# A selective-scan kernel: the positive part of softplus from half sums held in PSUM, and two copies, the sums' chain and the background pace moved

## The chip, the cores and the metric

The kernel runs on one core of a Trainium2 chip. A core has a matrix engine (TensorE, "PE" in the profile; its weight loads are "PEld"), a vector engine (VectorE, "DVE"), a scalar engine (ScalarE, "ACT"), GpSimd ("POOL"), and SyncE ("SP"), which issues the DMAs here. Each engine runs its own queue in order; semaphores make one wait for another. Matmuls write to PSUM, eight banks of 2 KB for each of 128 partitions; GpSimd and DMAs work on SBUF alone in this kernel. The metric is the device time of one execution in microseconds (us), lower is better.

## The reference, cut to what matters

The input is 16 images of 64 x 64 pixels with 96 channels. Layer 0 normalizes, upsamples with a Fourier filter, applies a 96 to 384 to 96 network with a quadratic activation and goes back. Layer 1 is a four-directional selective scan over the pixels, and nearly all of the time is its scan:

```
xz = x @ in_proj_w.T;  xc, z = split(xz);  z = silu(z)
xc = silu(conv3x3(xc))                       # depthwise
x_dbl = einsum(xs, x_proj_weight)            # 4 directions: dts (6), Bs (16), Cs (16) a pixel
dts   = einsum(dts, dt_projs_weight)
delta = softplus(dts + dt_projs_bias)
h_t   = exp(delta_t * A) * h_(t-1) + (delta_t * u_t) * B_t      # 16 states a channel
y_t   = sum over states of h_t * C_t, plus u_t * D
out   = layernorm(y over directions) * z, projected
```

The change touches `delta`: softplus(s) = max(s, 0) + ln(1 + exp(-|s|)).

## The kernel before, in words

The whole program is one long list of instructions whose order is written out by hand. First `front(0)` (layer 0 and the convolutions of image 0) runs by itself, then `scan()` runs over all 16 images, then `finish(15)` by itself. Inside `scan()`, the `front` of the next image and the `finish` of the image before (norm, gate and projection) are dealt out in small pieces, as background.

**Units.** An image has 8 steps: 4 pieces of 1024 pixels forward (`pair` 0), then the same 4 backward (`pair` 1). A step has 6 blocks (`bi`), a block has 4 units (`j`). So there are 192 units an image and 3072 in all. A unit has two halves, `e` = 1 ("odd") and `e` = 0 ("even"), each of 128 partitions x 1024 pixels (32 channels x 4 states). For unit n the loop in `scan()` emits, in this order:

- the odd scan `recur(n, 1)` on VectorE (L836 forward, L838 backward), then for j < 3 the next odd decay, `decay(n + 1, 1)`: exp(delta x A) on ScalarE (L821) into the PSUM tile `da1`
- `slot(0)`: position 0
- for j = 3 the odd half's product with C on VectorE (L968), the copy of the last state (L844) and the odd decay; for j < 3 that product on GpSimd (L977)
- the issue of the stores of `yt`, if a block has ended
- the drive b = (delta u) B of unit n + 2 on GpSimd (L827)
- the even scan `recur(n, 0)`, in place in the PSUM tile `da0`
- `read_out(n - 1)`: the sum over states on TensorE (L861, 8 matmuls a half) into the one PSUM bank `y`; a backward block starts that bank with L853
- `slot(1)`: position 1
- the even half's product on VectorE (L988), the copy of the state on ScalarE (L844), the next even decay `decay(n + 1, 0)` on ScalarE, which reuses `da0` and so waits for L988
- when unit n - 1 ended a block: `store(n - 1)` copies `y` to `yt` on ScalarE (L872)
- `slot(2)`: position 2

So a block has 12 positions (3 slots x 4 units), numbered 0 to 11. Each slot calls one piece of `block_work` and then at most one step of the background.

**The sums.** `block_work` runs one `task` a block. It makes `delta` and `dtu` = delta x u for 512 pixels. L683 multiplies `dtw_s` with `pr`, giving s in the PSUM tile `s`. ScalarE makes e = exp(-|s|) (L686, L687), m = relu(s) (L689), w = 1 + e (L690), d = ln(1 + e) (L692), and then w = 1 - w (L694), which puts back what 1 + e lost in rounding. Four identity matmuls (L699) add w, e, d and m in a new tile `s`. VectorE multiplies it by u (L703), ScalarE copies it to `delta` (L705), and both go to memory (L706, L708). Positions: L683 at 0, L686 and L687 at 1, L689 and L690 at 2, L692 at 3, L694 at 4, L699 at 6, L703 at 9, L705 and the first store at 10, the second at 11. With `late=1`, which the blocks 3 and 4 have, L683 is at 1, everything up to L699 one place later (so L699 is at 7), and L703 at 9 as ever.

In the blocks 2 and 3 three `u` tiles are fetched at position 6, and `mix` (L661) multiplies them into the PSUM tile `pp` at position 11; `mixed` (L666) copies it to `pr` at position 0 of the next block, ahead of that position's other work. `pp` and both `s` share the one bank of the pool `gps`.

**Background.** `Background` hands out a step when its count is behind the pace: `SLICES` steps over the image's 576 positions for `front`, then, once `front` has ended, `finish` of the image before with `FINISH` as its count over the positions left, less 6. A `WAIT` holds a step back until position 2 of a unit with j = 2. Counted in the code: `front` has 383 steps and ends at position 449; `finish` has 114 and takes the 120 positions after that. `finish` first loads y, then makes eight passes over 512 pixels of 13 steps each, every pass with 18 matmuls (L557 to L610) and three products on VectorE (L579, L590, L606).

PSUM is full: two banks for the background, four for `da1` and `da0`, one for `y`, one for `gps`.

Of the kernel before, what the change touches and what calls it, by code (L numbers as in the profile page):

```python
# [45 lines left out]
F32 = mybir.dt.float32  # L46
AF = mybir.ActivationFunctionType
# [23 lines left out]
POS = 3 * 8 * 6 * NQ  # L71
SLICES = 540
FINISH = 117
WAIT = -1
# [3 lines left out]
def tile_two_blocks(  # L78
# [30 lines left out]
    nc.sync.dma_start(out=zwt_s, in_=inpt[:, DI:2 * DI])  # L109

    one_s = const.tile([128, 1], F32, name="one_s")
    nc.gpsimd.memset(one_s, 1.0)
# [87 lines left out]
    def norm(xt):  # L200

        s = small.tile([C, 8], F32, name="gs")
        for t in range(8):
            junk = piece([C, TB], "junk")
            nc.scalar.activation(junk, xt[:, TB * t:TB * t + TB], AF.Identity, accum_out=s[:, t:t + 1])
            if t % 2:
                yield
        yield
# [7 lines left out]
        for t in range(8):  # L216
            junk = piece([C, TB], "junk")
            nc.scalar.activation(
                junk, xt[:, TB * t:TB * t + TB], AF.Square, bias=nmean, accum_out=s2[:, t:t + 1]
            )  # L220
            if t % 2:
                yield
        yield
# [301 lines left out]
    def finish(mi):  # L525
# [15 lines left out]
        ahead = fetch_y(0)  # L541
        for _ in range(2):
            yield
        tail = None
        for t in range(8):
# [7 lines left out]
            for ob, n in ((0, 128), (1, 64)):  # L553
                oc = slice(128 * ob, 128 * ob + n)
                y_ps = bank([n, 8, HW], "yc")
                for i, (w, of) in enumerate(((pmat_s[:, 0, oc], y0), (pd_s[:, 0, oc], u0), (pd_s[:, 1, oc], yu))):
                    nc.tensor.matmul(  # L557
                        y_ps, lhsT=w, rhs=of.rearrange("c (h w) -> c h w", w=HW), start=(i == 0), stop=False
                    )
                    if i == 1:  # L560
                        yield
                if tail is not None:
# [63 lines left out]
    def scan():  # L626


        with ExitStack() as es:
# [42 lines left out]

            def task(st, k, ps, make, late=0):

# [4 lines left out]
                u = fetch_u(st, v, t)  # L679
                for _ in range(late):  # L680
                    yield
                s = ps.tile([128, TB], F32, name="s", tag="g")
                nc.tensor.matmul(s, lhsT=dtw_s[:, pair, v, :], rhs=ctx["pr"][t], start=True, stop=True)  # L683
                yield
                e, d, m, w = (make(k) for k in ("e", "d", "m", "w"))
                nc.scalar.activation(e, s, AF.Abs)  # L686
                nc.scalar.activation(e, e, AF.Exp, scale=-1.0)  # L687
                yield
                nc.scalar.activation(m, s, AF.Relu)  # L689
                nc.scalar.activation(w, e, AF.Identity, bias=one_s)  # L690
# [4 lines left out]
                yield  # L695
                yield
                s = ps.tile([128, TB], F32, name="s", tag="g")
                for i, of in enumerate((w, e, d, m)):
                    nc.tensor.matmul(s, lhsT=ident_s, rhs=of, start=(i == 0), stop=(i == 3))  # L699
                for _ in range(3 - late):  # L700
                    yield
                dtu, delta = make("dtu"), make("delta")
                nc.vector.tensor_mul(dtu, s, u)  # L703
                yield
                nc.scalar.copy(delta, s)  # L705
                nc.sync.dma_start(out=ctx["dtu"][v][:, t:t + TB], in_=dtu)  # L706
                yield
                nc.sync.dma_start(out=ctx["delta"][v][:, t:t + TB], in_=delta)  # L708
# [4 lines left out]
            def block_work(st, bi, mi):  # L713
                more = st + 1 < len(steps)
                work = iter(())
                if bi < 3:
                    work = task(st, bi + 3, gps, near)
                elif more:
                    work = task(st + 1, bi - 3, gps, near, 1 if bi < 5 else 0)
                for p in range(3 * NQ):  # L720
                    if p == 0 and more and bi in (3, 4):
                        mixed(st + 1, *mixing.pop())
                    next(work, None)
                    if more and bi in (2, 3):
                        if p == 6:
                            if bi == 2:
                                if steps[st + 1][0] > mi:
                                    ahead_gen.drain()
                                open_step(st + 1)
                            us = [fetch_u(st + 1, v, TB * (bi - 2)) for v in range(3)]  # L730
                        elif p == 11:
                            mixing.append((TB * (bi - 2), mix(st + 1, us, gps)))
                    yield
# [179 lines left out]
            ahead_gen = behind_gen = nothing  # L913
            work, mixing = iter(()), []

# [16 lines left out]
            for n, (st, bi, j) in enumerate(units):  # L932
# [31 lines left out]
                if not odd_here:  # L964
                    decay(n + 1, 1)
                slot(0)
                if odd_here:
# [27 lines left out]
                slot(2)  # L995
# [126 lines left out]
```

## Time and profile before

| | |
|---|---|
| median of 3 runs | 20484.95 us (20470.02 to 20487.27) |
| the profiled execution | 20473.08 us |
| its span, first to last instruction | 20471.3 us |
| mean granted TensorE clock | 0.873 |
| DMA | 4478.55 MB, mean 219 GB/s |

The largest groups of instructions by line, with count, busy time and mean duration:

| line | engine, work | count | busy us | mean ns |
|---|---|---|---|---|
| L827 | GpSimd, drive b, 128 x 2048 | 3072 | 13903.4 | 4538 |
| L836, L838 | VectorE, scans, 128 x 1024 | 6144 | 14294.2 | 2280 to 2342 |
| L821 | ScalarE, decays, 128 x 1024 | 6144 | 6868.4 | 1118 |
| L977 | GpSimd, odd products, 128 x 1024 | 2304 | 5456.2 | 2368 |
| L988 | VectorE, even products | 3072 | 3760.5 | 1224 |
| L861 | TensorE, read-out, 128 x 256 | 49152 | 4161.1 | 421 to 427 |
| L699 | TensorE, four sums, 128 x 512 | 6136 | 3647.1 | 597 to 775 |
| L703 | VectorE, dtu | 767 | 521.6 | 680 |
| L689 | ScalarE, relu | 767 | 451.9 | 589 |
| L872 | ScalarE, copy of y | 768 | 444.8 | 579 |
| L705 | ScalarE, copy of the sums | 767 | 444.1 | 579 |

How to read the profile: a group's line gives busy time, mean of one instruction, and the idle time of its engine just before such instructions, with the engine and line that ended that idle time (the releaser). A line of waits reads "engine tile line <- releaser: total us, times, longest us". A line of the timeline gives start, duration, engine, line, operation, output<-inputs, and in brackets the idle time before it. A row of windows gives, for a stretch of the span, the busy time of each engine, then the granted clock, the DMA share and GB/s. Each matmul of this 4-byte data is two rows, so counts of matmuls are double; rows of matmuls overlap in time. Idle time of an engine that nobody waits for costs nothing. The columns of a busy row are engine, busy us, share of the span, and instructions.

### The profile page before, as it was taken

The numbers are of one execution on the slowest core, as the hardware profiler recorded it, in microseconds if no ns is written. First come the engines' busy times: TensorE is split into PE (matmuls) and PEld (weight loads), VectorE is DVE, ScalarE is ACT, GpSimd is POOL, SyncE is SP. The second block draws the span as 40 slices with busy tenths as digits, with TensorE's granted clock in tenths as the row PEclk, the third lists the DMA queues.
The fourth block names the chain that finished last, engine by engine and source line by source line (L and its number), as shares of the span: only waits on it lengthen the run. The fifth ranks groups of instructions, "written<-read, shape, count | busy, mean of one in ns | idle before, by whom it ended". The sixth has DMA issues, their size and how long they took to land. (4 is left out here: it accounts for less than half of the span.)

```text
span 20471.3 us, 274485 instructions
## 1 busy us (share of the span) xinstructions
PE 16699.0 (82%) x98988; PEld 7171.0 (35%) x98988; DVE 19208.3 (94%) x12989; ACT 13815.5 (67%) x20694; POOL 19150.8 (94%) x5384
## 2 busy tenths in 40 slices
PE   7877888888888878788887888888887787888767
PEld 4423334343333433334233343433334333242222
DVE  0999999999999999999999999999999999999997
ACT  4676767667676776766767676676767767677554
POOL 0999999999999999999999999999999999999996
PEclk8888898988889889888888889888898888888888
DMA  2666666766667676666766667667676666766664
GB/s 85 212 224 208 223 234 211 242 214 222 231 218 239 210 240 220 217 235 214 235 218 221 234 215 238 218 220 234 217 237 210 234 223 216 238 217 232 221 214 157
DMA packets 1966064, 4478.55 MB, mean 219 GB/s; under 512 B 461726, under 2 KB 560958, under 8 KB 1962654
## 3 DMA queue, kind: packets, MB, share of 16 engines
q1 hardware_dynamic: 1964702, 4461.00, 64.5%
q8 instruction: 781, 12.80, 0.3%
q14 instruction: 581, 4.76, 0.1%
HBM read 3581.91 MB, written 878.18 MB: 218 GB/s over the span
## 5 line engine op out<-in xcount | busy, mean ns | idle before, releaser
L827 POOL TENSOR_TENSOR b<-dtu,bt 128x2048 f32<-128x2048 f32 x3072 | 13903.4, 4538 | 471.7 <-DMA dtu<-dtu_d 467.9
L821 ACT ACTIVATE da<-delta,a_s 128x1024 f32<-128x1024 f32 x6144 | 6868.4, 1118 | 2264.3 <-DVE b L988 849.7
L977 POOL TENSOR_TENSOR odd<-b,ct 128x1024 f32<-128x1024 f32 x2304 | 5456.2, 2368 | 679.3 <-DVE b L836 246.2
L988 DVE TENSOR_TENSOR b<-da,ct 128x1024 f32<-128x1024 f32 x3072 | 3760.5, 1224 | 41.8
L836 DVE TENSOR_TENSOR_SCAN da<-da,new,b 128x1024 f32<-128x1024 f32 x1440 | 3372.8, 2342 | 82.6 <-ACT da L821 78.9
L838 DVE TENSOR_TENSOR_SCAN da<-da,new,b 128x1024 f32<-128x1024 f32 x1440 | 3370.2, 2340 | 15.8 <-ACT da L821 14.7
L861 PE MATMUL y<-b,fold_s 128*32 128x256 f32 x30720 | 2561.2, 427 | 797.7 <-ACT yt L872 411.5
L844 ACT COPY new<-da 128x1 f32<-128x1 f32 x2880 | 457.1, 159 | 2434.9 <-DVE b L988 1892.3
L836 DVE TENSOR_TENSOR_SCAN b<-da,new,b 128x1024 f32<-128x1024 f32 x864 | 2023.8, 2342 | 29.3 <-ACT da L821 28.3
L838 DVE TENSOR_TENSOR_SCAN b<-da,new,b 128x1024 f32<-128x1024 f32 x864 | 2022.5, 2341 | 29.2 <-ACT da L821 29.2
L487 PE MATMUL c_ps<-xgp,wtap_s 96*64 96x512 f32 (+1 forms) x4608 | 1764.7, 640 | 77.7 <-ACT row L505 71.9
L861 PEld LDWEIGHTS y<-b,fold_s 128*32 128x32 f32 x30720 | 739.7, 114 | 2919.4 <-issue 1557.0
L861 PE MATMUL y<-odd,fold_s 128*32 128x256 f32 x18432 | 1599.9, 421 | 197.3 <-POOL odd L977 197.0
L683 PE MATMUL s<-pr,dtw_s 128*128 128x512 f32 x1536 | 1034.5, 761 | 689.9 <-ACT delta L705 574.0
L661 PE MATMUL pp<-u,xpt_s 128*128 128x512 f32 x1536 | 891.7, 726 | 461.4 <-ACT delta L705 319.1
L699 PE MATMUL s<-w,ident_s 128*128 128x512 f32 x1534 | 1054.0, 775 | 238.4 <-ACT w L694 211.5
L370 PE MATMUL h_ps<-xu,w1t_s 96*128 96x500 f32 x1920 | 1038.8, 642 | 166.1 <-ACT hsq L351 121.1
L836 DVE TENSOR_TENSOR_SCAN da<-da,b 128x1024 f32<-128x1024 f32 x480 | 1096.2, 2284 | 79.2 <-ACT da L821 75.1
L838 DVE TENSOR_TENSOR_SCAN da<-da,b 128x1024 f32<-128x1024 f32 x480 | 1095.2, 2282 | 10.7 <-ACT da L821 9.2
L382 PE MATMUL o_ps<-w2c_s,hsq 128*100 128x96 f32 x9600 | 1009.2, 263 | 71.6 <-ACT hsq L351 71.3
L382 PEld LDWEIGHTS o_ps<-w2c_s,hsq 128*100 128x100 f32 x9600 | 946.0, 176 | 266.2 <-ACT hsq L351 111.4
L487 PEld LDWEIGHTS c_ps<-xgp,wtap_s 96*64 96x64 f32 (+1 forms) x4608 | 631.8, 177 | 1081.2 <-issue 942.6
(140 smaller groups left out, 23002.7 us busy)
## 6 DMA issues: line engine op xcount, KB each, us to landing
dtu<-dtu_d SPq DMA_DIRECT2D x1536, 512.0 KB
delta<-delta_d SPq DMA_DIRECT2D x1536, 512.0 KB
bt<-rows SPq DMA_DIRECT2D x1024, 512.0 KB
ct<-rows SPq DMA_DIRECT2D x1024, 512.0 KB
u<-xs_d SPq DMA_DIRECT2D x1664, 256.0 KB
dtu_d<-dtu SPq DMA_DIRECT2D x767, 256.0 KB
delta_d<-delta SPq DMA_DIRECT2D x767, 256.0 KB
xr<-in_x SPq DMA_DIRECT2D x768, 128.0 KB
```

Of the source, the lines that this page charges most:

```text
L370: nc.tensor.matmul(h_ps[j], lhsT=w1t_s[:, 128 * j:128 * (j + 1)], rhs=xu.rearrange("c p q -> c (p q)"), start=True, stop=True,)
L382: nc.tensor.matmul(o_ps[:, p, :], lhsT=hsq[j][:, UPS * p:UPS * (p + 1)], rhs=w2c_s[:, j, :], start=(j == 0), stop=(j == HB - 1),)
L487: nc.tensor.matmul(c_ps[p:p + n], lhsT=wtap_s[:, tap, 128 * i:128 * i + n], rhs=xgp[:, h0:h0 + 8, dx:dx + HW], start=(tap == 0), stop=(tap ...
L683: nc.tensor.matmul(s, lhsT=dtw_s[:, pair, v, :], rhs=ctx["pr"][t], start=True, stop=True)
L699: nc.tensor.matmul(s, lhsT=ident_s, rhs=of, start=(i == 0), stop=(i == 3))
L821: nc.scalar.activation(da, deltas[n // NQ, e], AF.Exp, scale=a_s[:, k, g, units[n][2]:units[n][2] + 1])
L827: nc.gpsimd.tensor_mul(b, dtus[n // NQ], bt.unsqueeze(1).to_broadcast([128, 2, T]))
L836: nc.vector.tensor_tensor_scan(out, da, b, before, ALU.mult, ALU.add)
L838: nc.vector.tensor_tensor_scan(out[:, ::-1], da[:, ::-1], b[:, ::-1], before, ALU.mult, ALU.add)
L861: nc.tensor.matmul(y[32 * q:32 * q + 32, e, :], lhsT=fold_s, rhs=weighed[e][:, QT * q:QT * q + QT], start=(pair == 0 and j == 0 and e == 0 ...
L977: nc.gpsimd.tensor_mul(odds[n], h, bc[1, r, j])
L988: nc.vector.tensor_mul(bs[n][:, 0, :], h, bc[1, r, j])
```

## The change

The positive part is made without Relu: `dtw_s` is halved at the start, so that L683 leaves s/2 in its bank, and the bank stays open. ScalarE makes m = |s| from it (with a scale of 2), then e from m. The four matmuls add to the same bank: 0.5 x m (through `half_s`, half an identity), w, e and d. s/2 + |s|/2 is max(s, 0), so the total is the same `delta`, in the order m, w, e, d.

All tasks have the same positions now: L683 at 0, Abs and Exp at 2, w at 3, d at 4, 1 - w at 5, the four matmuls at 6, the product at 9 with ScalarE's copy of the sums right behind it, both stores at 10. The `u` tiles for `mix` are fetched at position 3, `mix` stands at 10, `mixed` at 11 of the same block.

At the first unit of a block, `read_out(n - 1)` stands ahead of `slot(0)`, and the copy of `y` stands behind `slot(1)`, ahead of the even product, the state's copy and the even decay. In the other units both are where they were.

In the background, the two passes of the norm hand out one piece of 512 pixels a step and not two, `finish` waits 8 steps and not 2 for its first load and has two fewer steps in each pass (11 for 13), and the paces are 570 and 107. Counted in the code, `front` now has 399 steps and ends at position 461; `finish` has 104 and takes the 108 positions after that, at the pace 107 over 111 (before: 117 over 123).

```diff
-SLICES = 540
-FINISH = 117
+SLICES = 570
+FINISH = 107
...
+    half_s = const.tile([128, 128], F32, name="half_s")
+    nc.vector.tensor_scalar(half_s, ident_s, 0.5, None, ALU.mult)
+    nc.vector.tensor_scalar(dtw_s, dtw_s, 0.5, None, ALU.mult)
...
             nc.scalar.activation(junk, xt[:, TB * t:TB * t + TB], AF.Identity, accum_out=s[:, t:t + 1])
-            if t % 2:
-                yield
+            yield
...
         ahead = fetch_y(0)
-        for _ in range(2):
+        for _ in range(8):
             yield
...
                         y_ps, lhsT=w, rhs=of.rearrange("c (h w) -> c h w", w=HW), start=(i == 0), stop=False
                     )
-                    if i == 1:
-                        yield
...
-            def task(st, k, ps, make, late=0):
+            def task(st, k, ps, make):
...
-                for _ in range(late):
-                    yield
                 s = ps.tile([128, TB], F32, name="s", tag="g")
-                nc.tensor.matmul(s, lhsT=dtw_s[:, pair, v, :], rhs=ctx["pr"][t], start=True, stop=True)
+                nc.tensor.matmul(
+                    s, lhsT=dtw_s[:, pair, v, :], rhs=ctx["pr"][t], start=True, stop=False, skip_group_check=True
+                )
                 yield
                 e, d, m, w = (make(k) for k in ("e", "d", "m", "w"))
-                nc.scalar.activation(e, s, AF.Abs)
-                nc.scalar.activation(e, e, AF.Exp, scale=-1.0)
-                yield
-                nc.scalar.activation(m, s, AF.Relu)
+                yield
+                nc.scalar.activation(m, s, AF.Abs, scale=2.0)
+                nc.scalar.activation(e, m, AF.Exp, scale=-1.0)
+                yield
                 nc.scalar.activation(w, e, AF.Identity, bias=one_s)
...
-                yield
-                s = ps.tile([128, TB], F32, name="s", tag="g")
-                for i, of in enumerate((w, e, d, m)):
-                    nc.tensor.matmul(s, lhsT=ident_s, rhs=of, start=(i == 0), stop=(i == 3))
-                for _ in range(3 - late):
+                for by, of in ((half_s, m), (ident_s, w), (ident_s, e), (ident_s, d)):
+                    nc.tensor.matmul(s, lhsT=by, rhs=of, start=False, stop=(of is d), skip_group_check=True)
+                for _ in range(3):
                     yield
                 dtu, delta = make("dtu"), make("delta")
                 nc.vector.tensor_mul(dtu, s, u)
-                yield
                 nc.scalar.copy(delta, s)
+                yield
                 nc.sync.dma_start(out=ctx["dtu"][v][:, t:t + TB], in_=dtu)
-                yield
                 nc.sync.dma_start(out=ctx["delta"][v][:, t:t + TB], in_=delta)
...
-                    work = task(st + 1, bi - 3, gps, near, 1 if bi < 5 else 0)
+                    work = task(st + 1, bi - 3, gps, near)
                 for p in range(3 * NQ):
-                    if p == 0 and more and bi in (3, 4):
-                        mixed(st + 1, *mixing.pop())
                     next(work, None)
                     if more and bi in (2, 3):
-                        if p == 6:
+                        if p == 3:
...
+                        elif p == 10:
+                            pp = mix(st + 1, us, gps)
                         elif p == 11:
-                            mixing.append((TB * (bi - 2), mix(st + 1, us, gps)))
+                            mixed(st + 1, TB * (bi - 2), pp)
...
                 if not odd_here:
                     decay(n + 1, 1)
+                if n >= 1 and j == 0:
+                    read_out(n - 1)
                 slot(0)
...
-                if n >= 1:
+                if j > 0:
                     read_out(n - 1)
                 slot(1)
+                if n >= 1 and j == 0:
+                    storing = store(n - 1)
+                    next(storing)
                 nc.vector.tensor_mul(bs[n][:, 0, :], h, bc[1, r, j])
                 keep(n, 0, h, nc.scalar.copy)
                 if n < last:
                     decay(n + 1, 0)
-                if n >= 1 and units[n - 1][2] == NQ - 1:
-                    storing = store(n - 1)
-                    next(storing)
                 slot(2)
```

More of the change, by code (lines that the diff above doesn't have):

```diff
@@ L220, in norm @@
             )
-            if t % 2:
-                yield
+            yield
         yield
@@ L703, in task @@
                 nc.vector.tensor_mul(dtu, s, u)
+                nc.scalar.copy(delta, s)
                 yield
-                nc.scalar.copy(delta, s)
                 nc.sync.dma_start(out=ctx["dtu"][v][:, t:t + TB], in_=dtu)
-                yield
                 nc.sync.dma_start(out=ctx["delta"][v][:, t:t + TB], in_=delta)
@@ L913, in scan @@
             ahead_gen = behind_gen = nothing
-            work, mixing = iter(()), []
+            work = iter(())
             def slot(position):
```

## The prediction

> **What bounds the kernel now.** The first view is the page's busy table.
>
> ```profile
> PE 16699.0 (82%) x98988; PEld 7171.0 (35%) x98988; DVE 19208.3 (94%) x12989; ACT 13815.5 (67%) x20694; POOL 19150.8 (94%) x5384
> ```
>
> VectorE and GpSimd share the bound. GpSimd's 19150.8 us over 3072 units are 6.23 us a unit. The scans of VectorE's timeline (two to a unit) begin at 473.6 us and end at 20304.3 us: 6.457 us a unit, 1240 us an image of 192 units. Stretches without any wait (the units 72 to 88 of an image) run at 6.20, GpSimd's pace. So VectorE's waits are what can be won, but not whole: (1240 - 192 x 6.20 - 16) / 42.6 = 0.79, where 42.6 us is VectorE's waiting per image by the same walk (waits over 0.12 us; 634 us in all) and 16 us are `finish`'s 24 products of about 0.67. I count 0.8 us won per us of wait removed.
>
> Walking VectorE's instructions, the 634 us split so: before `dtu` (L703) 286, of which 236 in the blocks 3 and 4, the two whose task runs with `late=1`; before scans 343, of which 132 in block 3; `yz` 5. (The page's 456 us at L703 has one wait of 159.9 us in it, before the first scan.) The waits by pairs say who is late:
>
> ```profile
> PE s L683 <- ACT delta L705: 574.0, 218, 5.0
> DVE dtu L703 <- PE s L699: 455.1, 226, 159.9
> ...
> PE y L861 <- ACT yt L872: 411.5, 112, 7.9
> ...
> PE y L853 <- ACT yt L872: 341.2, 120, 6.4
> ...
> PE pp L661 <- ACT delta L705: 319.1, 123, 4.6
> ...
> DVE da L836 <- ACT da L821: 154.0, 149, 3.5
> ```
>
> The columns are total, times, longest. TensorE stands for 574 + 412 + 341 + 319 = 1646 us behind ScalarE's two late copies, `delta` and `yt`; all its gaps over 0.3 us inside the loop are 3608. VectorE pays when TensorE's late sums reach it. One late block in the timeline:
>
> ```profile
> 10831.50 0.71 ACT L694 ACTIVATE w<-w,one_s 128x512 f32<-128x512 f32 x1
> ...
> 10832.82 2.31 PE L382 MATMUL o_ps<-w2c_s,hsq 128*100 128x96 f32 x12 [0.38 <-ACT hsq L351]
> ...
> 10835.07 1.08 PE L861 MATMUL y<-b,fold_s 128*32 128x256 f32 x8
> 10835.13 2.35 DVE L836 TENSOR_TENSOR_SCAN da<-da,new,b 128x1024 f32<-128x1024 f32 x1
> ...
> 10836.92 1.13 PE L699 MATMUL s<-w,ident_s 128*128 128x512 f32 x2
> ...
> 10840.66 0.69 DVE L703 TENSOR_TENSOR dtu<-s,u 128x512 f32<-128x512 f32 x1 [3.18 <-PE s L699]
> ```
>
> `w` was done at 10832.2, but the four sums stand at position 7, behind `o_ps` and y, and begin at 10836.9; VectorE waits 3.18 us.
>
> **The change, part by part.** *The late chain (A).* All tasks get their sums at position 6. In the block above they would start their first matmul by about 10830.5, wait for `w` until 10832.2 and end by 10832.2 + 3 x 0.86 + 1.0 = 10835.8, ahead of the scan's end at 10837.5. Of the 236 us, 73 lie in `finish`'s stretch (counted below); of the other 163 I take 85%: -139 (bounds -163 and -80).
>
> *Delta copied behind the product, pp, pr and s one place earlier; y copied early (B).* Block 3's scan waits: by the longest ScalarE gap ahead of the late decay, 55 us hang on `pr`<-`pp` and 58 on `yt`. The delta copy stood behind the odd decay, which waits for L968: product's end + 1.21 + 1.12 + 0.58. Now it ends 0.58 behind the product, and `pp` stands at position 10. `yt` stood behind the even decay (L988's end + 1.12 + 0.58); now it runs in the time in which ScalarE waits for L988, and its matmuls are ahead of two positions' background work. Of 132: -95 (bounds -125, and 0 if `yt` then waits for a late TensorE with the even decay behind it: that decay has 2.34 - 1.12 = 1.2 us to spare).
>
> *The new wait.* In the built program every delta copy waits for VectorE's product. Behind it on ScalarE stand position 9's background step, the state copy and the odd decay; these two wait for L968 (1.21 us) anyway, so 0.58 of copy and some 0.6 of background are covered. The decay has the even scan and product to spare, 2.34 + 1.22. If `dtu` is late, it stands ahead of L968 in VectorE's own queue, so ScalarE's decay was late before too. Zero; without the cover 0.58 x 768 x 0.8 = 356.
>
> The Trainium skill (PSUM — Partial Sum Buffer, section "PSUM bank collisions raise a hardware error") says that two engines may not touch one bank at once, readers included, which speaks against copying beside the product. In this trace the copy's only listed wait is 13.2 us behind the product. By the rule the copy adds its 0.58 after the product rather than beside it, and the sum stays as it is, since it is covered either way.
>
> *Relu gone.* 767 x 589 ns = 452 us of ScalarE at 67%: off the path, zero by itself. Both matmul counts stay 5; `m` goes first and needs no `w`.
>
> *Shorter way from `w` to the sums.* In the blocks 0, 1, 2 and 5 `w` moves from position 4 to 5 with the sums still at 6: `w` ends about 1.12 + 0.72 after L988, the sums 3.4 us after, `dtu` is due 2.34 x 3 + 1.22 = 8.2 after L988. Three us to spare; but at half clock (below) a matmul takes 1.87 and the spare is gone. Between 0 and 512 x 0.8 x 0.25 = 100 us; I take +10, as the rows at full clock are three quarters of the span.
>
> *Other waits (C).* 266 us (50 at `dtu`, 211 at scans, 5 at `yz`), each at a fixed place of the image, from background steps in which ScalarE waits for TensorE. The pace of `front` changes (399 steps by position 461 for 383 by 449), so all coincidences fall anew; the norm's steps carry one pass of 0.7 and not two. TensorE's 1646 us of gaps shrink. Bounds -130 and +130; I take -80. A rule bears on this:
>
> ```profile
> core 0: us, PE busy (x) PEld busy (x) DVE busy (x) ACT busy (x) POOL busy (x), PEclk, DMA share, GB/s
> 10130.00:10144.00 14.00, 8.26 (x23) 2.91 (x24) 13.96 (x10) 10.05 (x15) 14.00 (x5) 0.51 1.03 267
> ...
> 10190.00:10351.00 161.00, 157.44 (x657) 50.49 (x656) 158.12 (x108) 97.99 (x136) 148.52 (x42) 0.98 0.75 246
> ```
>
> After two gaps of 3.75 and 4.33 us (for `delta`, then for y's load) the granted clock was 0.51 for these 14 us, and matmuls of 0.86 took 1.87. Gaps of 1.3 to 2.5 us stand before other drops in the trace. The Trainium skill (TensorE: Matmul & The Clock Gate, section "What's actually happening") lets the clock fall after an idle window of about 3.4 us; the removed gaps average 1646 / 573 = 2.9, so by it most would give no clock back and C would be nearer -40.
>
> *`finish` gets denser (D), the part that speaks against the change.* Its eight passes take 11 steps for 13; they run over 8 x 11 x 111/107 = 91 positions, 30.4 units, where they had 8 x 13 x 123/117 = 109, 36.4 units. In 10190 to 10351 (24 units, 5.27 passes) TensorE was busy 157.4 of 161. Own work there is about 2.6 a unit (read-out 1.0, a fourth of five matmuls of 0.9, `pp` and y's start 0.45), so a pass costs (157.4 - 62.4) / 5.27 = 18.0 and all eight 144. After: 144 + 30.4 x 2.6 = 223 us; VectorE needs only 30.4 x 6.2 + 16 = 205. By spacing of matmul starts (0.86) TensorE's need is about 7% below its busy time, 207. I take 215. The units 150 to 192 took 283 us (10119.7 to 10403.2); after: 215 + 11.6 x 6.25 = 287.5, which has the waits of A's 73 and y's load (4.3 us, now covered by eight steps for two) inside. +4.3 x 15 images = +65; bounds 205 (-90) and, at 95% use of 230, +290.
>
> Sum: (-139 - 95 - 80) x 0.8 + 10 + 65 = -176 against the profiled span of 20471.3 (its run took 20473.1; ends before the first scan and after the last stay). The median is 12 us above that run: 20,485 - 176 = **20,310**.
>
> **Rivals.** *Waits change place:* C turns to +130 and D to 223 (+12 x 15 = 180): -187 + 104 + 10 + 180 = +107 at worst, about 0 in the middle: 20,490. For it: 42 us an image come from fixed coincidences, and all are dealt again. Against: A and B are tied to their blocks. *TensorE bounds `finish` (slower):* 223 at 92% use, as in 10133 to 10190 (52.67 of 57), is 242: 315 for 283, +31 x 15 = 470, with the rest 20,485 - 241 + 470 = 20,710; at 240 it is 20,680. It decides from 215 + 176/15 = 227 us on. For it: TensorE is busy 98% there already. Against: VectorE hardly waits there (158.1 of 161), so TensorE's busy time isn't all need. *Nothing shortened:* if the sums at position 6 wait for `w` as long as they waited for their place, A goes and C halves: 20,485 - (95 + 40) x 0.8 + 75 = 20,450.
>
> **How the numbers follow.** Forecast 0.64; waits change place 0.12; TensorE-bound `finish` 0.20; nothing shortened 0.04. A difference under 0.2% (41 us) can't be told from none. Likeliest case's own range: A, B, C, D at their good ends give 20,485 - 334 - 90 = 20,060, at half of A and B 20,440. For 8 in 10 I take 20,090 to 20,600, which leaves out the good end of D and the worse half of the slower rival. Faster: the forecast and some of the last two, 0.67; within 0.2%: 0.11; slower 0.22.
>
> **What would show it.** `dtu` waits in the blocks 3 and 4 outside `finish` under 30 us; `s`<-`delta` and `y`<-`yt` under 250 together; granted clock above 0.873; units 150 to 192 in 280 to 295 us. Wrong if those last take over 300, if new `dtu` waits stand in blocks 0, 1, 2 or 5, or if the even decay waits behind `yt`.

## The result, and the profile after

The changed kernel takes 20671.62 us (median of 4 runs, 20667.13 to 20686.19) against 20477.49 (20468.05 to 20487.27) for the kernel before in the same comparison: 1.0096 times as long, 95% interval 1.0079 to 1.0113. It is slower by 194 us. The profiled execution took 20667.13 us, its span is 20665.3, and the mean granted clock 0.865 (before 0.873).

The busy row of the changed kernel's page:

```profile
PE 16816.0 (81%) x98988; PEld 7255.0 (35%) x98988; DVE 19227.3 (93%) x12991; ACT 13435.2 (65%) x19926; POOL 19146.1 (93%) x5384
```

VectorE and GpSimd have the work they had (19 and 5 us apart from before), and ScalarE has 380 us less; TensorE has 117 us more for as many instructions, at the lower clock. So the bounding engines got no more to do; the time is waiting. Its waits by pairs (total us, times, longest):

```profile
PE s L696 <- ACT w L693: 948.6, 284, 5.4
...
ACT delta L701 <- DVE dtu L700: 530.7, 261, 8.9
...
DVE dtu L700 <- PE s L696: 377.7, 157, 157.1
...
PE y L849 <- DMA y<-part: 237.7, 42, 14.1
DVE da L832 <- ACT da L817: 236.0, 225, 2.2
...
PE y L849 <- ACT yt L868: 64.0, 45, 2.5
...
PE pp L660 <- ACT delta L701: 23.2, 32, 1.8
```

These rows say two things. The last two: what the change set out to remove is gone. TensorE stood 1646 us behind `delta` and `yt`, and now 64 + 23. The first rows: TensorE now stands 949 us at the sums for w (212 before), and the `dtu` waits fell only from 455 to 378, 157 to 160 of it the first one in both kernels. And a new row: y's start, L849, waits for the load of `part`, 238 us in 42 times, at most 14.1.

Where in an image the time went is read from VectorE's scans, as mean over the images 2 to 13 (us per image), with VectorE's waits over 0.12 us in the same stretch:

| stretch | before | after | waits before: scans, `dtu`, finish | waits after |
|---|---|---|---|---|
| units 0 to 150 | 960.2 | 954.3 | 18.9, 13.3, 0.0 | 19.5, 6.4, 0.0 |
| units 150 to 192 (`finish`) | 284.0 | 303.8 | 1.8, 6.8, 0.4 | 5.2, 10.3, 12.0 |

So the loss is in `finish`: +19.8 us an image, and the front part gains a mere 5.9. Some 14 us an image over the 15 images with a `finish` in the loop are 210 us, about the loss of 194.

**How finish starts.** SyncE's queue of the changed kernel around the loads for `finish` of image 6 (start, duration, line, output<-input):

```profile
10225.08 0.34 SPq L200 DMA_DIRECT2D ycol<-y_d  x1
10225.74 0.53 SPq L753 DMA_DIRECT2D bt<-rows  x1
10226.40 0.52 SPq L753 DMA_DIRECT2D ct<-rows  x1
...
10235.65 0.48 SPq L200 DMA_DIRECT2D ycol<-y_d  x1
...
10239.44 0.34 SPq L536 DMA_DIRECT2D y<-y_d  x1
...
10243.59 0.45 SPq L538 DMA_DIRECT2D yu<-y_d  x1
...
10245.11 0.53 SPq L762 DMA_DIRECT2D y<-part  x1
```

The timeline of the same place (in brackets the idle time before, and who ended it):

```profile
10244.50 2.34 DVE L834 TENSOR_TENSOR_SCAN b<-da,new,b 128x1024 f32<-128x1024 f32 x1
...
10251.47 2.04 PE L849 MATMUL y<-y,ident_s 128*128 128x512 f32 x2 [13.57 <-DMA y<-part]
...
10255.49 2.35 POOL L975 TENSOR_TENSOR odd<-b,ct 128x1024 f32<-128x1024 f32 x1 [6.56 <-PE y L857]
...
10259.15 0.69 DVE L700 TENSOR_TENSOR dtu<-s,u 128x512 f32<-128x512 f32 x1 [6.54 <-PE s L696]
...
10259.88 0.59 ACT L701 COPY delta<-s 128x512 f32<-128x512 f32 x1 [8.19 <-DVE dtu L700]
```

The scan at 10244.50 is that of unit 158. The six loads of `ycol` (512 KB each) and the four loads of y and u that `finish` issues stand in the one queue among the loads of B (`bt`) and C (`ct`), and `part`, which a backward block needs to start y, leaves the queue behind them, 0.6 us after that scan began. It is there 6.36 us later. TensorE runs in order, so all stands behind L849: the read-out, the sums behind it, and then GpSimd 6.56 us, VectorE 6.54 and ScalarE 8.19. This repeats: the `dtu` wait of unit 159 is 6.46 us in the mean, in 14 images.

The load of y itself is no longer late. Before, TensorE waited for it in 14 images and in the last `finish`; in the changed kernel it does so only in the last one, behind the loop (the second row):

```profile
PE yc L557 <- DMA y<-y_d: 82.3, 15, 18.4
```

```profile
PE yc L558 <- DMA y<-y_d: 19.2, 1, 19.2
```

**How finish runs.** One of its products in the timeline after:

```profile
10345.45 2.07 PE L569 MATMUL yc<-ycol,pmat_s 128*128 128x512 f32 x4
...
10347.56 0.60 ACT L565 ACTIVATE sq<-yc 128x512 f32<-128x512 f32 x1 [4.76 <-PE yc L569]
...
10348.19 0.69 DVE L578 TENSOR_TENSOR yz<-yc,z 128x512 f32<-128x512 f32 x1 [1.85 <-ACT sq L565]
```

TensorE comes late with `yc`, ScalarE waited 4.76 us for it, VectorE then 1.85 in its own queue, with scans behind it. The rows of windows (stretch, its length, then busy us of PE, PEld, DVE, ACT and POOL with counts, granted clock, DMA share, GB/s):

```profile
10244.00:10267.00 23.00, 15.54 (x58) 5.53 (x58) 14.88 (x12) 7.00 (x12) 16.25 (x5) 0.75 0.88 281
...
10300.00:10443.00 143.00, 140.31 (x574) 46.16 (x574) 130.94 (x89) 79.64 (x107) 124.73 (x35) 1.00 0.72 235
```

In the first 23 us TensorE, VectorE and GpSimd stand for a third of the time: the late start. In the long stretch TensorE is busy 98% at full clock and VectorE 130.94 of 143, 92%. VectorE waits there behind TensorE, as in the rows above; the runs at other densities, below, show that TensorE bounds it.

### The profile page after: what moved, and what is told of

Same layout as the page of the kernel before. It is cut to its first block, busy times and chain, and to the rows that moved or that the text cites. A ratio compares the mean times of both kernels' runs of the same rounds, so it can differ in the third digit from the quotient of the medians.

```text
span 20665.3 us, 274460 instructions
## 1 busy us (share of the span) xinstructions
PE 16816.0 (81%) x98988; PEld 7255.0 (35%) x98988; DVE 19227.3 (93%) x12991; ACT 13435.2 (65%) x19926; POOL 19146.1 (93%) x5384
## 3 DMA queue, kind: packets, MB, share of 16 engines
q14 instruction: 581, 4.76, 0.1%
## 5 line engine op out<-in xcount | busy, mean ns | idle before, releaser
L488 PE MATMUL c_ps<-xgp,wtap_s 96*64 96x512 f32 (+1 forms) x4608 | 1661.0, 620 | 76.9 <-ACT row L506 71.1
L383 PE MATMUL o_ps<-w2c_s,hsq 128*100 128x96 f32 x9600 | 1097.4, 277 | 77.4 <-ACT hsq L352 77.2
L383 PEld LDWEIGHTS o_ps<-w2c_s,hsq 128*100 128x100 f32 x9600 | 1037.7, 189 | 305.0 <-issue 139.1
L680 PE MATMUL s<-pr,dtw_s 128*128 128x512 f32 x1536 | 1067.8, 784 | 71.4 <-ACT pr L665 70.3
L696 PE MATMUL s<-m,half_s 128*128 128x512 f32 x1534 | 1035.8, 763 | 52.0 <-ACT m L686 51.0
```

What stands on the lines that cost most here:

```text
L383: nc.tensor.matmul(o_ps[:, p, :], lhsT=hsq[j][:, UPS * p:UPS * (p + 1)], rhs=w2c_s[:, j, :], start=(j == 0), stop=(j == HB - 1),)
L488: nc.tensor.matmul(c_ps[p:p + n], lhsT=wtap_s[:, tap, 128 * i:128 * i + n], rhs=xgp[:, h0:h0 + 8, dx:dx + HW], start=(tap == 0), stop=(tap ...
L696: nc.tensor.matmul(s, lhsT=by, rhs=of, start=False, stop=(of is d), skip_group_check=True)
```

## The experiments

All of these compute the whole reference. Stretch times are us per image as above; "positions a pass" is how far the background spreads one of `finish`'s eight passes.

| run | median us | ratio to before [95%] | units 0 to 150 | 150 to 192 |
|---|---|---|---|---|
| before | 20477 to 20495 | 1 | 960.2 | 284.0 |
| after | 20671.62 | 1.0096 [1.0079, 1.0113] | 954.3 | 303.8 |
| e1_chain_only | 20151.15 | 0.9832 [0.9817, 0.9847] | 941.9 | 279.0 |
| e2_background_only | 20914.83 | 1.0205 [1.019, 1.022] | 966.1 | 310.2 |
| e3_finish_old | 20547.93 | 1.0029 [1.0018, 1.004] | 953.1 | 296.2 |
| e4_w_earlier | 20680.08 | 1.0091 [1.0076, 1.0106] | 952.8 | 304.7 |
| e5_pace_570 | 20241.08 | 0.9883 [0.9869, 0.9898] | 950.3 | 277.3 |
| e6_y_as_before | 20209.01 | 0.9868 [0.9853, 0.9883] | 946.6 | 278.9 |
| e7_delta_later | 20286.25 | 0.9904 [0.9887, 0.992] | 950.2 | 281.3 |
| e8_relu | 20254.07 | 0.9889 [0.9875, 0.9904] | 948.0 | 279.6 |
| e9_w_on_chain | 20146.78 | 0.9836 [0.9822, 0.9851] | 943.9 | 276.8 |
| e10_finish_new | 20202.71 | 0.9864 [0.9849, 0.9878] | 944.1 | 281.4 |
| e11_finish_denser | 20344.41 | 0.9934 [0.9918, 0.9951] | 943.8 | 291.8 |
| e12_places_only | 20396.92 | 0.9957 [0.9942, 0.9972] | 957.3 | 280.3 |
| e13_start_449 | 20344.50 | 0.993 [0.9915, 0.9945] | 943.3 | 291.7 |
| e14_start_449_sparse | 20202.51 | 0.986 [0.9844, 0.9876] | 944.5 | 281.1 |

### The two halves apart

**e1_chain_only**: the changed kernel with the background of before.

```diff
-SLICES = 570
-FINISH = 107
+SLICES = 540
+FINISH = 117
...
-            yield
+            if t % 2:
+                yield
...
-        for _ in range(8):
+        for _ in range(2):
             yield
...
+                    if i == 1:
+                        yield
```

> The changed kernel with all its background edits undone (norm two pieces a step, finish with 2 waiting steps and 13 steps a pass, paces 540 and 117); the sums' chain, the copies of the sums and of y stay changed. By the walk of VectorE's scans an image's units 150 to 192 take 284.0 us before and 303.8 after the change, and its units 0 to 150 take 960.2 and 954.3. Theory 1, the denser finish is the loss: units 150 to 192 come back to 280 to 288, the run takes 20,340 to 20,450, faster than the kernel before. Theory 2, the chain is the loss (w one position from its sums, or the copy of y ahead of the even decay): units 150 to 192 stay at 298 or more and the run takes over 20,600.

Measured 20151.15: 334 us below before (20485), 520 below the change. The chain's half is a clear gain, and the version beats both kernels. Its waits by pairs, and its row of windows for the dense part of `finish`:

```profile
PE s L700 <- ACT w L697: 809.7, 270, 6.0
...
DVE dtu L704 <- PE s L700: 218.6, 88, 156.9
...
DVE da L836 <- ACT da L821: 120.2, 129, 2.0
```

```profile
10022.00:10183.00 161.00, 156.75 (x669) 51.16 (x662) 157.25 (x106) 95.14 (x131) 150.46 (x43) 1.00 0.75 245
```

Less the first wait of 156.9, `dtu` waits 62 us in the whole run, where it waited 295 before and 221 after. In `finish` TensorE has slack (97%) and VectorE is busy 98%. TensorE's 810 us behind w are there too, in the best kernel, so that row of the changed kernel is no explanation.

**e2_background_only**: the kernel before with the reverse of that diff.

> The kernel before with the background edits alone (norm one piece a step, finish with 8 waiting steps and 11 steps a pass, paces 570 and 107). Theory 1: units 150 to 192 take 300 us or more and the run 20,700 to 20,850, since the old chain's waits come on top. Theory 2: units 150 to 192 take 280 to 290 and the run 20,420 to 20,560.

Measured 20914.83: the background edits cost 426 us on the old chain, 520 on the new one. Both halves are large, of opposite sign, and not quite additive.

**e3_finish_old**: the changed kernel with `finish` as before (two waiting steps, 13 steps a pass, FINISH 117), the new norm and pace 570 kept, so that it still starts at 461.

```diff
-FINISH = 107
+FINISH = 117
...
-        for _ in range(8):
+        for _ in range(2):
             yield
...
+                    if i == 1:
+                        yield
```

> The changed kernel with the old finish alone: 2 waiting steps, 13 steps a pass, 114 steps, which now run one at every position from 461 on (104 positions, 34.7 units for the eight passes; 30.4 in the changed kernel, 36.4 before). Theory 1 with TensorE's need of 223 us in that stretch: 34.7 units need 144 + 34.7 x 2.6 = 234 us of TensorE and 231 of VectorE, so units 150 to 192 take 286 to 294 and the run 20,450 to 20,560. If not the density but the merged step of three matmuls and the longer wait of 8 steps are the loss, they come back to 284 and below.

Measured 20547.93. A sparser `finish` (13.0 positions a pass) wins 124 us, but 397 us of the loss on e1 stay. In 14 images VectorE stands 8.7 us in the mean at `yz` of unit 158, behind TensorE waiting for `finish`'s own load of y: with two steps of notice the late load is met directly. So density is one part, and something in the start another.

**e4_w_earlier**: the changed kernel with Abs and Exp at position 1, w at 2, d at 3, 1 - w at 4; the sums stay at 6. It was to test whether the row of 949 us behind w costs anything.

```diff
                 e, d, m, w = (make(k) for k in ("e", "d", "m", "w"))
-                yield
                 nc.scalar.activation(m, s, AF.Abs, scale=2.0)
...
                 nc.scalar.activation(w, w, AF.Identity, scale=-1.0, bias=one_s)
                 yield
+                yield
```

> The changed kernel with Abs to 1 - w one position earlier each (Abs and Exp at 1, w at 2, d at 3, 1 - w at 4; the sums stay at 6). TensorE's gaps before the sums behind w, 942 us in the changed kernel and 229 before, fall under 300. Theory 1: that is no loss by itself outside finish, the run takes 20,600 to 20,700. Theory 2 in the form of w: the run falls by over 100 us, under 20,570.

Measured 20680.08, 8 us from the change: nothing. The largest row of TensorE's waits is worth nothing.

### The chain's parts, each undone on e1

**e6_y_as_before**: `read_out` and the copy of `y` go back to their old places.

```diff
-                if n >= 1 and j == 0:
-                    read_out(n - 1)
                 slot(0)
...
-                if j > 0:
+                if n >= 1:
                     read_out(n - 1)
                 slot(1)
-                if n >= 1 and j == 0:
-                    storing = store(n - 1)
-                    next(storing)
...
                     decay(n + 1, 0)
+                if n >= 1 and units[n - 1][2] == NQ - 1:
+                    storing = store(n - 1)
+                    next(storing)
```

> The chain-only kernel with the read-out and the copy of y at a block's first unit back in their old places. If the early copy carries a good part of the chain's 338 us: TensorE's waits for yt, about 750 us before, come back above 500 and the run takes 20,230 to 20,350. If it carries nothing: 20,110 to 20,190.

Measured 20209.01, +58 on e1. Its waits show the old pair back, a little above its old size (753 us):

```profile
PE y L861 <- ACT yt L872: 496.8, 124, 7.6
PE y L853 <- ACT yt L872: 366.7, 167, 6.6
```

So 863 us of TensorE's standing were worth 58 us.

**e7_delta_later**: ScalarE's copy of the sums one position behind the product, as before.

```diff
                 nc.vector.tensor_mul(dtu, s, u)
-                nc.scalar.copy(delta, s)
                 yield
+                nc.scalar.copy(delta, s)
                 nc.sync.dma_start(out=ctx["dtu"][v][:, t:t + TB], in_=dtu)
```

> The chain-only kernel with ScalarE's copy of the sums one position later (10 for 9), behind the odd decay as before; pp stays at 10 and now stands in the same position as the copy. If the copy's place carries a good part: TensorE's waits for delta before pp and s come back above 300 us and the run takes 20,230 to 20,350. If not: 20,110 to 20,190.

Measured 20286.25, +135 on e1, with this row back among the waits:

```profile
PE pp L664 <- ACT delta L706: 329.0, 219, 4.1
```

329 us of standing here are worth 135, 0.41 us each, where y's copy gave 0.07. VectorE's own waits say why: in the units 0 to 150 those before scans rise from 12.2 to 17.8 us an image and those before `dtu` from 2.6 to 4.5, with y's copy undone (e6_y_as_before) to 13.8 and 4.8.

**e8_relu**: the old arithmetic in the new places: `dtw_s` whole, Relu one position behind Exp, a fresh tile `s` for four whole identity matmuls.

```diff
-    nc.vector.tensor_scalar(dtw_s, dtw_s, 0.5, None, ALU.mult)
...
-                nc.scalar.activation(m, s, AF.Abs, scale=2.0)
-                nc.scalar.activation(e, m, AF.Exp, scale=-1.0)
+                nc.scalar.activation(e, s, AF.Abs)
+                nc.scalar.activation(e, e, AF.Exp, scale=-1.0)
                 yield
+                nc.scalar.activation(m, s, AF.Relu)
...
-                for by, of in ((half_s, m), (ident_s, w), (ident_s, e), (ident_s, d)):
-                    nc.tensor.matmul(s, lhsT=by, rhs=of, start=False, stop=(of is d), skip_group_check=True)
+                s = ps.tile([128, TB], F32, name="s", tag="g")
+                for of in (m, w, e, d):
+                    nc.tensor.matmul(s, lhsT=ident_s, rhs=of, start=(of is m), stop=(of is d))
```

> The chain-only kernel with the old arithmetic (Relu from s, a new tile for the four sums with the whole identity, dtw not halved), all positions as changed, Relu at 3 with w. ScalarE does 452 us more. By my prediction that is off the path: 20,110 to 20,190. If ScalarE's time counts where its decays are late: 20,220 to 20,320.

Measured 20254.07, +103 on e1. VectorE's waits before scans in the units 0 to 150 rise from 12.2 to 17.1 us an image, those before `dtu` only from 2.6 to 3.0. 767 Relus of 589 ns on an engine busy 67% of the span are then hardly free: the decays that the scans wait for stand behind them in ScalarE's queue. (The fresh tile `s` comes back with this edit too and was not run apart; that the wait grew before scans, whose decays ScalarE makes, speaks for Relu but doesn't prove it.)

**e9_w_on_chain**: e4's edit on e1.

> The chain-only kernel (20,151 us) with Abs to 1 - w one position earlier each. TensorE's gaps before the sums behind w fall from 802 us to under 300. If those gaps lie where TensorE has time to spare, as the same edit on the changed kernel said (20,680 for 20,672): 20,110 to 20,190. If they cost: under 20,090.

Measured 20146.78, 4 us from e1. TensorE's gaps before the sums' w fall from 802 us to 215, and those before the read-out's rows of `b` rise from 1155 to 1598: the engine waits for the next thing. TensorE's waits by themselves are not time.

**e12_places_only**: the kernel before with the task's new positions alone (no `late`, sums at 6 in every block, fetch at 3, `pp` at 10, `pr` at 11); Relu, the late `delta` copy, y's places and the background stay as before.

> The kernel before with the chain's places alone (no late tasks, sums at 6, u tiles at 3, pp at 10, pr at 11; delta copied at 10, y's copy, Relu and the background as before). The three other parts of the chain were worth 58 (y), 135 (delta) and 103 us (Relu) when each was taken out of the chain-only kernel; of its 338 us that leaves about 42 for the places. If the parts add up: 20,400 to 20,480. If the places carry the gain and the rest only keeps it: under 20,340. By my prediction's term A (139 x 0.8): 20,375.

Measured 20396.92, 84 us below the shared runs of before. The `dtu` waits fall from 20.1 to 7.8 us an image, and those before scans rise from 20.7 to 25.1.

Taken one by one the four parts are 84 + 58 + 135 + 103 = 380, against 334 together.

### The background's parts

**e5_pace_570**: e1 with SLICES 570 alone; the front then ends at 437.

```diff
-SLICES = 540
+SLICES = 570
```

> The chain-only kernel (20,151 us; its units 0 to 150 take 941.9 us and 150 to 192 take 279.0) with front at the pace 570 and nothing else of the background: front ends at position 437, finish gets 132 positions, 14.8 a pass. Units 0 to 150 took 953 to 954 in both kernels with the new norm and 570. Theory 1a, the denser pace of front makes that: 950 to 956 here, and with finish at 277 to 280 the run takes 20,270 to 20,370. Theory 1b, the norm's single pieces make it: 940 to 944 and the run 20,080 to 20,180.

Measured 20241.08, +90 on e1: +8.4 us an image in the units 0 to 150, and `finish`, with more positions, 1.7 less.

**e10_finish_new** and **e11_finish_denser**: e1 with the new `finish` (8 waiting steps, 11 steps a pass), which starts at 449; FINISH 107 gives 12.6 positions a pass, 118 gives 11.5. The diff of the second against e1:

```diff
-FINISH = 117
+FINISH = 118
...
-        for _ in range(2):
+        for _ in range(8):
             yield
...
-                    if i == 1:
-                        yield
```

> The chain-only kernel with the new finish (8 waiting steps, 11 steps a pass, 107): it starts at position 449 as before, so its six loads of y come ahead of the rows' loads (bt, ct) of units 151 to 156, with 12.6 positions a pass (13.7 in the chain-only kernel, 11.4 in the changed one). Its units 150 to 192 take 279.0 in the chain-only kernel, 303.8 in the changed one. Theory 1c, the late start (461) is the larger part of the loss, since the loads of y and part land late behind the rows' loads and TensorE stands 13.6 us: 276 to 283, the run 20,110 to 20,210, TensorE's waits for part under 100 us. Theory 1, density: 284 to 290, the run 20,220 to 20,320.

> The same with 118 in place of 107: start at 449, 11.5 positions a pass, the density of the changed kernel without its late start. Theory 1c: units 150 to 192 at 284 or less, the run under 20,230. Theory 1, density with TensorE at its bound (223 us of need in 30.4 units): 290 to 297, the run 20,310 to 20,420, with waits at yz and dtu in units 171 to 187 as in the changed kernel.

Measured 20202.71 and 20344.41. With the start kept, 13.7 positions a pass (e1) give 279.0 us for the units 150 to 192, 12.6 give 281.4, 11.5 give 291.8. The price is not linear: 2.4 us for the first position taken away, 10.4 for the next. The change has 11.4 and 303.8, so 12 us an image were still without a cause but the start, compared across kernels that differ in the front too.

**e13_start_449** and **e14_start_449_sparse** test that within the changed kernel itself.

```diff
-SLICES = 570
-FINISH = 107
+SLICES = 600
+FINISH = 118
```

> The changed kernel with SLICES = 600 and FINISH = 118: the front then ends at position 449 instead of 461, and finish takes 109 positions for its 104 steps, 11.5 a pass, as dense as in the changed kernel (11.4). Late start theory (finish that starts at 461 has its loads of y and part queued behind the loads of B and C, and that costs about 12 us an image): the units 150 to 192 take about 292 us as in the denser finish on the new chain, not 304, and the dtu wait of unit 159 (6.46 us in every image) is gone. Density theory (11 steps a pass at this pace is the whole loss): they stay at about 304. The denser front costs by itself: 540 to 570 cost 8.4 us an image, so 954 may become 954 to 963. Run: 20,450 to 20,640 by the first, 20,670 to 20,810 by the second.

> The changed kernel with SLICES = 600 alone: finish starts at 449 and takes 120 positions, 12.6 a pass. Against the run before it only the density differs, against the changed kernel the start too. If both parts are real and add, the units 150 to 192 take about 281 us (as the new finish at 12.6 on the new chain did) and the run 20,290 to 20,480; if density is the whole loss, about 291 to 293 and 20,480 to 20,640; if the front at pace 600 gives it all back, the units 0 to 150 take over 970 and the run is over 20,550 in either case.

Measured 20344.50 and 20202.51 (the second keeps FINISH 107). At the same density, the start at 449 for 461 takes the units 150 to 192 from 303.8 to 291.7. By stretches of six units, 7.9 of these 12.1 us lie in the units 156 to 162, where TensorE stands for `part`, 3.4 in 174 to 180 and 3.2 in 186 to 192, into which `finish` reaches when it starts 12 positions later; the other stretches give back some 2. Why the two later stretches cost more was not taken apart, so the loads are shown as the cause of a good half of the 12.1 and not of all. SyncE's queue of e13_start_449:

```profile
10042.74 0.52 SPq L200 DMA_DIRECT2D ycol<-y_d  x1
...
10045.34 2.49 SPq L200 DMA_DIRECT2D ycol<-y_d  x4
...
10053.18 0.48 SPq L200 DMA_DIRECT2D ycol<-y_d  x1
...
10057.67 0.55 SPq L753 DMA_DIRECT2D bt<-rows  x1
...
10087.05 0.39 SPq L762 DMA_DIRECT2D y<-part  x1
```

and its timeline at unit 158, whose scan is the second row:

```profile
10093.34 1.12 PE L849 MATMUL y<-y,ident_s 128*128 128x512 f32 x2
...
10095.92 2.34 DVE L834 TENSOR_TENSOR_SCAN b<-da,new,b 128x1024 f32<-128x1024 f32 x1
```

The `ycol` loads leave 53 to 43 us ahead of that scan and ahead of the loads of B and C; in the changed kernel 19 to 9 us ahead, among them. `part` leaves 8.9 us ahead of it, not 0.6 behind, and here TensorE doesn't wait for it. The `dtu` wait of 6.46 us in unit 159 is gone. The density then shows by itself, in the rows of windows of e13_start_449 (11.5 a pass) and of e14_start_449_sparse (12.6):

```profile
10111.00:10290.00 179.00, 178.66 (x737) 58.11 (x736) 165.10 (x112) 101.30 (x140) 153.78 (x45) 1.00 0.71 229
```

```profile
10046.00:10210.00 164.00, 163.41 (x679) 53.69 (x677) 160.96 (x110) 98.62 (x134) 151.92 (x44) 1.00 0.75 243
```

TensorE is busy over 99% in both, but VectorE 92% in the first and 98% in the second. The busy share of TensorE doesn't tell the two apart; VectorE's does.

The units 0 to 150 brought a surprise: 943.3 and 944.5 at pace 600, where 570 with the same 399 steps gives 954.3 (after) and 953.1 (e3). A denser front that costs less: so the 8 to 11 us that pace 570 costs are not the price of density as such. That they come from where its steps fall among the chain's is what is left; it is argued, not shown. The largest differences from e13_start_449 are in the units 52 to 56 (28.6 us for 25.7), 68 to 72 (27.4 for 25.3) and 36 to 40 (29.7 for 28.0). Which step meets which there was not followed up.

The change therefore adds up so: before 20485; the chain -334 (e1); `finish` at 12.6 positions a pass +51 (e14_start_449_sparse, and e10_finish_new the same); at 11.5 +142 (e13_start_449, e11_finish_denser the same); pace 570 with the start at 461 +327. The sum is +186 for a measured +187 (194 against the runs of before in the same comparison). Of the 327, 12.1 us an image are in `finish` with its later start, 11.0 in the front with its pace; over 15 images that makes some 180 and 165, a little over the 327.

## Why the prediction was wrong, point by point

It said 20,310 and faster; measured was 20,672 and slower, above the 20,600 of its range. Of the 362 us between, the chain took 93 off by giving more than forecast. The step that failed is the price of the background edits: D put it at +65, and C counted the front's new pace among the gains. With the changed chain they cost 520: 193 by the density of `finish`, and 327 by its later start (some 180) and the front's pace (some 165).

- *The whole chain's part (A, B, C with the step w to the sums)* was forecast at (-139 - 95 - 80) x 0.8 + 10 = -241; measured -334. Right in sign, a quarter too small.
- *A, the tasks' places*: forecast -111, measured -84 (e12_places_only). The `dtu` waits of the blocks 3 and 4 outside `finish` fell from 168 us to 25 in the changed kernel, as it said (under 30), but the scans took part of it back.
- *B, delta's and y's copies*: forecast -95 x 0.8 = -76, measured 135 + 58 = 193 when they are undone one by one. Mis-sized: it looked for B's gain before the scans of block 3 alone (132 us). When `delta`'s copy is put back (e7_delta_later), the waits rise there by 41 us, but also by 33 before the scans of block 4 and by 59 before `dtu`.
- *Relu's end at nothing, "off the path"*: wrong, 103 us with the tile `s` that goes with it. ScalarE's busy share of 67% was taken for slack, yet scans wait for decays in its queue. How much is Relu and how much the tile wasn't taken apart.
- *The copy behind the product, a new wait, at nothing*: not contradicted. ScalarE waits 531 us there, and moving the copy out of it costs 135; the wait's own price was not measured apart from the gain of the earlier place. The Trainium skill (PSUM — Partial Sum Buffer, section "PSUM bank collisions raise a hardware error"), cited for this order, isn't contradicted: in the changed kernel's trace each of the 767 copies starts after its product has ended.
- *The shorter way from w to the sums, +10*: right in size. It made the 949 us row, and giving it a position back changes the time by 8 and by 4 us (e4_w_earlier, e9_w_on_chain).
- *0.8 us won per us of VectorE's wait*: too small. On e1 the waits fall by 22.5 us an image (41.2 to 18.7), the time by 23.3: one for one. The waits it divides by were read a little too large: the trace has 316 us before scans and not 343, which makes the 0.79 about 0.82.
- *C, as a gain from the other waits, -64*: this step failed. With 316 for 343 these waits were 239 us and not 266; outside the units 150 to 192 they were 196, are 172 with the chain alone (e1) and 285 in the changed kernel. That "all coincidences fall anew" was taken for a gain, and as a loss put into a rival at +130 at worst; the new deal of the units 0 to 150 at pace 570 cost 11.0 us an image, +165.
- *D, the denser `finish`*: the main failure. Its density was well sized: it gave 287.5 us for the units 150 to 192, and with the old start they take 291.7 (e13_start_449). That y's load is "now covered by eight steps for two" came true: inside the loop TensorE no longer waits for it. What failed is that the later start of `finish`, which the prediction named (461 for 449), was put at nothing in D. The 12 positions put ten loads among the loads of B and C in SyncE's one queue, and `part` behind them, for which TensorE now stands 238 us. The later start costs +12.1 us an image, 7.9 of it where `part` is late; the rest stays open. D came out at 303.8, +16.3 over its figure.
- *The rivals*: "TensorE bounds `finish`", at 20,680 to 20,710, hit the size, by chance in part. It had -241 for the rest and +31 us an image in `finish`; measured are +19.8 in `finish` and a rest of only -5.9 an image in the units 0 to 150. Its mechanism is shown (from 12.6 to 11.5 positions a pass VectorE falls from 98% busy to 92 behind a TensorE that has no room) and is about half of what `finish` lost on e1. "Waits change place" was right too, in the front, with a larger price than its +104.
- *What would show it*: `s` behind `delta` and `y` behind `yt` under 250 together was right (64). The granted clock above 0.873 was wrong (0.865). Of the signs of failure, the units 150 to 192 over 300 us came, and so did new `dtu` waits: in block 1 they rose from 4.7 us to 60.7, in block 5 from 4.7 to 27.2. With the chain alone (e1) they are 1.2 and 4.3, so the background makes them and not the shorter way from w. ScalarE is hardly late at `yt`: it waits 24 us ahead of its 768 copies.
- *A sum*: half of A and B, with the rest of the forecast, gives 20,400 and not 20,440.

## What to carry to other kernels

Cost an edit of pace by two things apart: how dense an in-order engine's work becomes (here 2.4 us an image from 13.7 positions a pass to 12.6, and 10.4 more to 11.5), and where its first loads then stand in the queue that issues them, against which other loads (7.9 us an image where `part` came behind them). When a change joins several edits, one run with each half tells at once whether a loss hides a gain: here -334 and +520, and undoing the second half gives 20151.15 us, 1.68% below before, the best found along with e9_w_on_chain. Rank waits by what the bounding engine waits for: 949 us of TensorE behind w were worth nothing, 329 behind `delta` were worth 135.

## What the runs showed of the hardware

- Behind the stand of 13.57 us the two rows of L849 take 2.04 us in the changed kernel; the same two, without the stand, 1.12 in e13_start_449. The granted clock is 0.50 from 10235.10 to 10255.50. The stand, which begins at 10237.90, didn't start this: the two rows of L680 at 10235.82 take 2.07 already, behind gaps of 1.19 and 2.69 us. The Trainium skill (TensorE: Matmul & The Clock Gate, section "What's actually happening") lets the clock fall after an idle window of about 3.4 us. Here it fell within the gap of 2.69 us, and stayed down through the stand.
- The mean granted clock doesn't rank the kernels: e5_pace_570 has 0.889 and takes 20241.08 us, e1_chain_only 0.877 and 20151.15.
- A load of 256 KB (`part`) was issued at 10245.11 and its matmul began at 10251.47, 6.36 us later, with the DMA engines at 0.88 of the time in that window. TensorE doesn't wait when it is issued 8.9 us ahead of the scan of unit 158; issued 0.6 after, VectorE waits 6.5 us.
